# Keys and values stored to DRAM in 64-byte pieces, sorted by the partition that reads them, and loaded as 2 KB rows; chunk matmuls in two-bank tiles

## The chip, the cores and the metric

The kernel runs on one core of a Trainium2 chip. The metric is the device time of a run in microseconds (us). A separate execution was taken by the hardware profiler; its span is the time from its first to its last instruction.

## The reference

All arithmetic is float32. x is [64 batches, 64 tokens, 256]. Four layers, each with a residual, follow one another:

```python
x = x + L0(x, cond)      # adapter 256 -> 64 -> 256, weights scaled and shifted per batch
x = x + L1(x, cond)      # per batch a 256 -> 30 -> 256 product, U decoded from cond
x = x + L2(x, cond)      # attention among the 16 heads of ONE token
x = x + L3(x, ids, ...)  # gathered layer norms, hidden layer with silu, layer norm

# L2
kx = modulated_linear(x, s, k_aff_w, k_aff_b, k_w, k_b).reshape(B, N, 16, 16)
q = k = v = kx                                            # [b, token, head, d]
scores = einsum('bnhd,bnjd->bnhj', q, k) / sqrt(16)
out = einsum('bnhj,bnjd->bnhd', softmax(scores), v).reshape(B, N, 256)
out = modulated_linear(out, s, o_aff_w, o_aff_b, o_w, o_b)

# L3
h = ln(ln(x, pw_g[p], pw_b[p]), cp_g[c], cp_b[c]);  t = ln(x, tm_g[c], tm_b[c]);  s = ln(x, ms_g[m], ms_b[m])
# three more branches add per-batch vectors to x
y = ln(silu(concat(6 weighted branches) @ int_W1 + int_b1) @ int_W2 + int_b2, int_g, int_be)
```

The attention is between the heads of one token: each token has its own 16 x 16 score matrix.

## The kernel before

The 4096 tokens are taken in 8 chunks of 512 (`layers01`: layers 0 and 1 and the keys) and 16 units P of 256 (`attention` and `layers23`). x is held feature-major, 2 x 128 features on the partitions.

`layers01` runs stages "down" (tile p1 in PSUM), "up" (pu, evacuated by 16 small ScalarE operations into t1; pr, from which VectorE makes t2), "mid" (py, pz), "park" (x is written to DRAM as xd) and "keys" (pk, evacuated by 16 ScalarE operations into kT). Stage "turn" transposes kT (pt), and ScalarE copies it twice into the tile kk: once with the heads innermost (for the keys), once plainly (for the values). kk goes to DRAM as kd (L663).

`fetch` loads what the attention matmuls read. Eight tokens share a 128 x 128 matmul, 16 partitions (one for each d or head) for each token. kb holds keys of 8 tokens side by side; kz holds the same keys with gaps of zeros, so that each block of the product stays apart; vb holds values. kb and kz come in 8 + 8 DMAs of 16 x 32 pieces of 64 B (L679), vb in 8 such DMAs (L685). kb and vb have one buffer each, kz has two. "scores" multiplies kz by kb into pS (L707), VectorE and ScalarE make the softmax (mx, E, sm, at), "values" multiplies at by vb into pv (L731). ScalarE copies pv into av, four DMAs store it as ad (L743), one loads it back feature-major as aT (L747).

`layers23` scales aT (aS), multiplies (po, L794), scales on ScalarE (ot, 8 operations, L797) and adds the residual to xr, which was read back from xd. px (L805) transposes to token-major; ScalarE copies it to xt; VectorE makes statistics and the normalised branches in the order xh, pw, pw, statistics of pw, cg, mg, pw. POOL raises the variances to -1/2 and issues the gathers. pft, pfs, pfh (L830) transpose back, ph (L841, L843) is the hidden layer, pq (L851) its output, then a last layer norm and out.

PSUM has eight banks: tag A with two single banks for the chunk's tiles (taken in a fixed turn), tag B with three for layers23, S one for pS, V two for pv.

No order is written by hand. Each operation is a step with an engine, a cost, what it reads and writes, and a rank; `Plan.order` lets a list scheduler with modelled costs choose the order: among the steps of an engine that could start within 0.25 us of the earliest, the one of lowest rank. A step's rank is its unit's due time (25 us per P) plus a lead per stage (`LEAD`). All plain DMAs but W_dec and two small loads are on the SP queue, which issues them in that order and waits in that order.

Of the kernel before, what the change touches and what calls it, by code (L numbers as in the profile page):

```python
# [10 lines left out]
AF = mybir.ActivationFunctionType  # L11
# [5 lines left out]
HB = 64  # L17
# [44 lines left out]
class Plan:  # L62
# [3 lines left out]
    LANES, ISSUE, LAND, RATE, HOP, SLACK = 8, 0.57, 2.0, 280e3, 0.12, 0.25  # L66
    TABLE = 1.28

    LEAD = {"down": -39.4, "up": -8.6, "mid": -59.6, "keys": 28.3, "turn": 3.2, "fetch": 58.2,
            "scores": 59.6, "values": 68.7, "out": 41.8, "norm": -8.5, "hidden": 52.2, "last": 114.8,  # L70
            "gather": 86.4, "park": 50.6, "load": 74.1, "load first": -172.8, "load decoder": 56.9, "load up": -37.6,
            "load keys": 86.0, "load ids": -10.1, "load W1": -27.4, "load states": 22.4, "load W2": 20.8, "set down": -180.7,
            "set decoder": 123.4, "set k": -104.6, "set o": 113.5, "set W1": -81.6, "set states": 97.6}

    def __init__(self):
        self.stage = None
        self.steps, self.bufs, self.turn = [], {}, {}
        self.last_w, self.last_r = {}, {}

# [10 lines left out]
    def step(self, eng, cost, fn, r=(), w=(), rank=0.0, dma=None, table=None):  # L90
# [16 lines left out]
        for seen, mine in ((self.last_w, writes), (self.last_r, reads)):  # L107
            for name, part in mine:
# [3 lines left out]
                               stage=self.stage))  # L112
# [7 lines left out]
    def order(self):  # L120
        steps = self.steps
        n = len(steps)
        for s in steps:
            s["rank"] = s["base"] + self.LEAD.get(s["stage"], 0.0)
        users = {i: [] for i in range(n)}
# [18 lines left out]
        while placed < n:  # L144
# [44 lines left out]
            if s["dma"] is not None:  # L189
                pipe = max(pipe, t + cost + 0.8) + s["dma"] / self.RATE  # L190
                done[i] = max(t + cost + self.LAND, pipe + 1.0)
                if e != "POOL":
                    lanes.append(done[i])
# [29 lines left out]
def act(n, k=1):  # L223
    return 0.20 * k + n / 1250.0
# [3 lines left out]
def tile_kernel(ctx: ExitStack, tc: tile.TileContext, a: dict, out: bass.AP):  # L228
# [11 lines left out]
    BUFS = {"x": 3, "xr": 3, "pw": 2, "cg": 2, "mg": 2, "ei": 2, "oh": 2, "t4": 3, "kk": 2, "act": 2, "E": 2,  # L240
# [5 lines left out]
    def bank(name, tag="A", turns=False):  # L246
        return Buf(ps, tag, {"A": 2, "B": 3, "S": 1}[tag], [128, 512], name, turns=turns)
# [16 lines left out]
    onesz = fixed("onesz", [128, 2, 128])  # L264
# [31 lines left out]
    kb, vb = (kv[:, i * NG * 128 : (i + 1) * NG * 128].rearrange("p (g b j) -> p g b j", g=NG, b=8) for i in range(2))  # L296
# [3 lines left out]
    def consts():  # L300
        make_identity(nc, ident)

    step("POOL", 1.0, lambda: (nc.gpsimd.memset(ones, 1.0), nc.gpsimd.memset(onesz, 0.0),
                               nc.gpsimd.memset(onesz[0:HB, 0, :], 1.0), nc.gpsimd.memset(onesz[HB:128, 1, :], 1.0)),
         w=["ones", "onesz"], rank=-109)
# [247 lines left out]
    kds, xds = {}, {}  # L553

    def layers01(c, rank):
# [6 lines left out]
        p1 = bank(f"p1_{c}", turns=True)  # L562

        def f():
            for i in range(2):
# [15 lines left out]
        pu = [bank(f"pu_{c}_{h}", turns=True) for h in range(2)]  # L581
        step("PE", 0.9, lambda: [mm(pu[h]()[:, d * 256 : (d + 1) * 256], up2[h * HB : (h + 1) * HB, d * 128 : (d + 1) * 128],
                                    ac()[h * HB : (h + 1) * HB, :], start=True, stop=True) for d in range(2) for h in range(2)],
             r=[ac, "up2"], w=pu, rank=rank)
        for h in range(2):
            step("ACT", 8 * 0.31, lambda h=h: [
                nc.scalar.activation(t1()[:, d, h * 256 + b * S : h * 256 + (b + 1) * S], pu[h]()[:, d * 256 + b * S : d * 256 + (b + 1) * S],
                                     AF.Copy, scale=ugT[:, d, b0 + h * PB + b : b0 + h * PB + b + 1])
                for d in range(2) for b in range(PB)], r=[pu[h], "ugT"], w=[(t1, h)], rank=rank)
        pr = bank(f"pr_{c}", turns=True)  # L590
        step("PE", 0.9, lambda: [mm(pr()[:, h * 256 : (h + 1) * 256], onesz[:, h, :], ac(), start=True, stop=True) for h in range(2)],
             r=[ac, "onesz"], w=[pr], rank=rank)
        t2 = sb("t4", [128, 2, CH], f"t2_{c}")
        step("DVE", vec(1024), lambda: nc.vector.tensor_tensor(
            bt(t2()), over(pr().rearrange("p (b s) -> p b s", s=S), 2), rep(ubT[:, :, b0 : b0 + CB], S), ALU.mult),
            r=[pr, "ubT"], w=[t2], rank=rank)
# [4 lines left out]
        py = bank(f"py_{c}", turns=True)  # L601
# [10 lines left out]
        for h in range(2):  # L612
# [4 lines left out]
        pz = [bank(f"pz_{c}_{h}", turns=True) for h in range(2)]  # L617
        step("PE", 0.9, lambda: [mm(pz[h]()[:, d * 256 : (d + 1) * 256], V[h * HB : h * HB + K1P, d * 128 : (d + 1) * 128],  # L618
                                    y()[h * HB : h * HB + K1P, :], start=True, stop=True) for d in range(2) for h in range(2)],
             r=[y, "V"], w=pz, rank=rank)  # L620
        for h in range(2):
            step("DVE", vec(512), lambda h=h: nc.vector.tensor_tensor(
                x()[:, :, h * 256 : (h + 1) * 256], x()[:, :, h * 256 : (h + 1) * 256], pz[h]().rearrange("p (d t) -> p d t", d=2), ALU.add),
                r=[pz[h]], w=[(x, h)], rank=rank)
# [9 lines left out]
        kT = sb("t4", [128, 2, CH], f"kT_{c}")  # L634
        for o in range(2):
            pk = bank(f"pk_{c}_{o}", turns=True)
            step("PE", 1.75, lambda o=o, pk=pk: [mm(pk(), wT["k"][:, k, o * 128 : (o + 1) * 128], xs()[:, k, :], start=(k == 0), stop=(k == 1))  # L637
                                                 for k in range(2)], r=[xs, "w_k"], w=[pk], rank=rank)
            step("ACT", 8 * 0.31, lambda o=o, pk=pk: [
# [303 lines left out]
```

## Time and profile before

| | us |
|---|---|
| median of 3 runs (lowest to highest) | 538.52 (536.18 to 541.24) |
| the profiled execution | 543.12 |
| its span | 541.3 |
| first pS (scores of P=0) starts | 85.53 |
| first pft (hidden layer of P=0) starts | 129.24 |
| last pft (hidden layer of P=15) starts | 516.32 |

The lines of a profile read as follows. An engine's line gives its busy time, the share of the span and the number of instructions (PE is TensorE, PEld its weight loads, DVE VectorE, ACT ScalarE, POOL GpSimd). A DMA queue's line gives packets, MB, and the time that the packets took as a share of 16 DMA engines over the span. A line of the waits names the waiting engine, tile and line, then what released it, then total us, number of times and the longest. A line of the timeline gives start, duration, engine, line, operation, out<-in, shape and count; in brackets stands the engine's idle time before it and what ended that. SPq is the SP queue: the duration is that of the issuing instruction. Matmuls are pipelined, so that neighbouring durations overlap slightly. Line numbers are those of the kernel before; the changed kernel numbers its lines anew.

### The profile page before, as it was taken

To read this page: it belongs to the slowest core of one execution; us is meant where nothing else is said; L and a number is where in the kernel's file an instruction comes from. 1 tells how busy PE (TensorE), PEld (TensorE's weight loads), DVE (VectorE), ACT (ScalarE), POOL (GpSimd) and SP (SyncE) were. 2 spreads that over 40 slices of the span, in tenths; PEclk is the share of its full clock that TensorE was granted. 3 is DMA by queue.
4 is the path that set the end of the run, shared out by engine and by line. 5 is a ranking of instruction groups with operands and counts; after the bars stand their busy time and mean duration, and the time that the engine had idled before them with its cause. 6 is when DMAs were issued, how large, how long until landed. Compare 5 with 4: busy or idle time off the path is not lost.

```text
span 541.3 us, 10927 instructions
## 1 busy us (share of the span) xinstructions
PE 437.3 (81%) x4026; PEld 345.4 (64%) x4026; DVE 356.6 (66%) x778; ACT 244.6 (45%) x624; POOL 164.6 (30%) x181
## 2 busy tenths in 40 slices
PE   4976879677996998699899987999798869676481
PEld 3874446556775867477677676867676758665370
DVE  1653755258658785866859886797879494775532
ACT  1301532452557364825755576466647535251210
POOL 5380310003451515141425151515142424430100
PEclk9955986877999899979899999999999979796877
DMA  8994593656987697778687877878696869731000
GB/s 291 307 222 143 171 114 34 164 66 91 219 196 146 137 148 177 160 143 157 181 154 157 137 181 138 159 129 198 118 167 112 203 132 135 138 95 53 0 19 19
DMA packets 256994, 77.30 MB, mean 143 GB/s; under 512 B 226130, under 2 KB 242542, under 8 KB 256942
## 3 DMA queue, kind: packets, MB, share of 16 engines
q1 hardware_dynamic: 249006, 51.59, 48.9%
q0 software_dynamic: 6656, 20.98, 17.0%
q10 hardware_dynamic: 1280, 4.05, 2.0%
q8 instruction: 32, 0.52, 0.4%
q14 instruction: 20, 0.16, 0.1%
HBM read 55.60 MB, written 20.97 MB: 141 GB/s over the span
## 4 chain that ended last, share of the span: by engine, by line
PE 41%; SPq 22%; DMA 13%; DVE 12%; issue 6%; ACT 4%; POOL 1%; POOLq 0%; DVEq 0%; ACTq 0%
PE ph L843 12%; SPq L679 11%; PE pS L707 5%; DMA kd<-kk 4%; SPq L685 4%; PE po L794 4%; PE pq L851 3%; SPq L743 3%; PE pz L618 2%; DMA kz<-kd 2%; DMA aT<-ad 2%; DMA aff_k<-in_k_aff_wT 2%; PE pk L637 2%; PE ph L841 2%; PE pv L731 2%
## 5 line engine op out<-in xcount | busy, mean ns | idle before, releaser
L707 PE MATMUL pS<-kv,kz 128*32 128x128 f32 x1024 | 43.9, 343 | 33.1 <-DMA kz<-kd 21.5
L707 PEld LDWEIGHTS pS<-kv,kz 128*32 128x32 f32 x1024 | 38.7, 140 | 41.4 <-issue 31.0
L797 ACT ACTIVATE ot<-po,cols,demod_o 128x64 f32<-128x64 f32 x128 | 39.6, 417 | 30.3 <-PE po L794 30.3
L767 POOL DMA_INDIRECT mg<-in_ms_tab,ids x32 | 34.4, 1076 | 48.7 <-PE pfs L830 25.0
L757 POOL TENSOR_TENSOR rs_y<-rs_y,neghalf 128x2 f32<-128x2 f32 x16 | 12.6, 787 | 111.0 <-DVE rs_y L756 111.0
L757 POOL TENSOR_TENSOR rs_x<-rs_x,neghalf 128x2 f32<-128x2 f32 x16 | 12.7, 796 | 108.2 <-DVE rs_x L756 108.2
L640 ACT ACTIVATE kT<-pk,cols,demod_k 128x64 f32<-128x64 f32 x128 | 38.7, 440 | 7.7 <-PE pk L637 4.5
L833 ACT COPY ft<-pft 128x512 f32<-128x512 f32 x16 | 9.4, 585 | 72.1 <-PE pft L830 72.1
L767 POOL DMA_INDIRECT pw<-in_pw_tab,ids x32 | 33.3, 1040 | 10.4 <-issue 9.1
L767 POOL DMA_INDIRECT cg<-in_cg_tab,ids x32 | 32.5, 1015 | 11.3 <-issue 8.7
L843 PE MATMUL ph<-ft,W_t 128*128 128x256 f32 x128 | 35.6, 403 | 0.0
L854 DVE TENSOR_TENSOR y<-pq,irow 128x512 f32<-128x512 f32 x16 | 11.0, 688 | 35.8 <-PE pq L851 35.8
L790 DVE TENSOR_TENSOR aS<-aT,style_o 128x512 f32<-128x512 f32 x16 | 11.1, 691 | 34.8 <-DMA aT<-ad 34.8
L757 POOL TENSOR_TENSOR rs_h<-rs_h,neghalf 128x2 f32<-128x2 f32 x16 | 16.8, 1051 | 56.1 <-DVE rs_h L756 56.1
L794 PE MATMUL po<-aS,w_o 128*128 128x256 f32 x128 | 32.7, 401 | 0.9 <-DVE aS L790 0.9
L843 PE MATMUL ph<-xr,W_x 128*128 128x256 f32 x128 | 33.4, 383 | 0.0
L843 PE MATMUL ph<-fh,W_h 128*128 128x256 f32 x128 | 32.9, 380 | 0.0
L843 PE MATMUL ph<-fs,W_s 128*128 128x256 f32 x128 | 32.9, 379 | 0.0
L851 PE MATMUL pq<-W,hs 128*128 128x256 f32 x128 | 31.1, 385 | 1.8 <-ACT hs L846 1.7
L830 PE MATMUL pft<-ident,cg 128*128 128x128 f32 x64 | 12.3, 324 | 24.4 <-DVE cg L818 16.4
L731 PE MATMUL pv<-kv,at 128*32 128x128 f32 x1024 | 31.3, 274 | 0.8 <-issue 0.8
L637 PE MATMUL pk<-xs,w_k 128*128 128x512 f32 x64 | 31.0, 629 | 0.0
(217 smaller groups left out, 1020.9 us busy)
## 6 DMA issues: line engine op xcount, KB each, us to landing
kd<-kk SPq DMA_DIRECT2D x16, 512.0 KB
kv<-kd SPq DMA_DIRECT2D x256, 32.0 KB
x<-in_xT SPq DMA_DIRECT2D x8, 512.0 KB
xd<-x SPq DMA_DIRECT2D x8, 512.0 KB
xr<-xd SPq DMA_DIRECT2D x16, 256.0 KB
kz<-kd SPq DMA_DIRECT2D x128, 32.0 KB
ad<-av SPq DMA_DIRECT2D x64, 64.0 KB
aT<-ad SPq DMA_DIRECT2D x16, 256.0 KB
```

Source lines behind the costliest of these rows:

```text
L637: step("PE", 1.75, lambda o=o, pk=pk: [mm(pk(), wT["k"][:, k, o * 128 : (o + 1) * 128], xs()[:, k, :], start=(k == 0), stop=(k == 1)) for ...
L640: nc.scalar.activation(kT()[:, o, b * S : (b + 1) * S], pk()[:, b * S : (b + 1) * S], AF.Identity, scale=demod["k"][:, o, b0 + b : b0 + b ...
L679: nc.sync.dma_start(dst, bass.AP(k.tensor, k.offset + (q * 64 + l) * 2 * D, [[NH, HD], [2 * 2 * D, NG], [1, NH]]))
L685: nc.sync.dma_start(vb[b * 16 : (b + 1) * 16, :, b, :], bass.AP(k.tensor, k.offset + b * 2 * D + D, [[HD, NH], [8 * 2 * D, NG], [1, HD]]))
L707: mm(pS()[32 * cc : 32 * cc + 32, r * 128 : (r + 1) * 128], kzt[:, g * 32 + 16 : g * 32 + 48] if h == 0 else kzt[:, g * 32 : g * 32 + 32], ...
L731: mm(pv()[32 * q : 32 * q + 32, r * 2 + h, :], at_[:, c0 : c0 + 32], vb[:, q * 8 + h * 4 + r, :, :].rearrange("p b d -> p (b d)"), start=T ...
L757: step("POOL", 0.7, lambda: nc.gpsimd.tensor_tensor(rs(), rs(), neghalf[:, 0:2], ALU.pow), r=["neghalf"], w=[rs], rank=rank)
L767: step("POOL", 1.2, lambda dst=dst, tab=tab, i=i, t=t: nc.gpsimd.indirect_dma_start(out=dst()[:, t, :], out_offset=None, in_=a[tab], in_of ...
L794: step("PE", 1.74, lambda: [mm(po()[:, o * PT : (o + 1) * PT], wT["o"][:, k, o * 128 : (o + 1) * 128], aS()[:, k, :], start=(k == 0), stop ...
L797: step("ACT", 4 * 0.31, lambda o=o: [nc.scalar.activation(ot()[:, o, b * S : (b + 1) * S], po()[:, o * PT + b * S : o * PT + (b + 1) * S], ...
L843: mm(dst(), W1[n][:, k, o * 128 : (o + 1) * 128], rhs()[:, k, :], start=False, stop=(n == "h" and k == 1))
L851: step("PE", 0.87, lambda t=t: [mm(pq()[:, t * D : (t + 1) * D], hs()[:, k, t * 128 : (t + 1) * 128], W2[:, k, :], start=(k == 0), stop=(k ...
```

## The change

- kd becomes [d, token, head] and a new tensor vd [token mod 8, head, group, d] takes the values. Six DMAs store them in 64 B pieces: two for kd (one for each half of the tokens), four for vd.
- `fetch` loads kd once as a whole (kc, 128 rows of 2 KB), from which a ScalarE copy fills kz; kb and vb take 8 DMAs each of 16 rows of 2 KB. kb and vb are laid out block-major, so the matmuls read their moving operand as 8 pieces of 16 elements. The order of the tokens within a unit changes accordingly, and av and ad with it: ad's pieces are 128 B instead of 256 B.
- The two A banks become one tile of two banks for pu, pr, pz and pk. p1, py and pt move to the three B banks. pr multiplies only the 64 rows that it needs for each half; t2 is made in two halves.
- The scheduler's costs are new, its DMA model counts pieces, all `LEAD` numbers are new, and a table `SHIFT` adds an offset for each stage and unit.

```diff
-    LEAD = {"down": -39.4, "up": -8.6, "mid": -59.6, "keys": 28.3, "turn": 3.2, "fetch": 58.2,
...
+    LEAD = {"down": 461.1, "fetch": 587.4, "gather": 700.5, "hidden": 385.3, "keys": 522.6, "last": 599.3,
...
+    SHIFT = {"down": (16.6, 0.0, 113.0, 0.0, 97.7, 0.0, 91.0, 0.0, -9.0, 0.0, 7.5, 0.0, 47.7, 0.0, 9.6, 0.0),
...
-    kb, vb = (kv[:, i * NG * 128 : (i + 1) * NG * 128].rearrange("p (g b j) -> p g b j", g=NG, b=8) for i in range(2))
+    kb, vb = (kv[:, i * NG * 128 : (i + 1) * NG * 128].rearrange("p (b g j) -> p b g j", g=NG, b=8) for i in range(2))
...
-        pu = [bank(f"pu_{c}_{h}", turns=True) for h in range(2)]
+        pu = banks(f"pu_{c}")
...
-        step("PE", 0.9, lambda: [mm(pr()[:, h * 256 : (h + 1) * 256], onesz[:, h, :], ac(), start=True, stop=True) for h in range(2)],
+        step("PE", 0.45, lambda: [mm(pr()[:, h, 0:PT], onesq[h * HB : (h + 1) * HB, :], ac()[h * HB : (h + 1) * HB, :], start=True, stop=True)
...
-            kd = kds[P] = Buf(dram, "kd", 2 * NC, [PT, 2, D], f"kd_{P}")
-            step("SP", Plan.ISSUE, lambda kk=kk, kd=kd: nc.sync.dma_start(kd().rearrange("(t p) i f -> p t i f", p=128), kk()),
+            kd = kds[P] = Buf(dram, "kd", 2 * NC, [HD, PT, NH], f"kd_{P}")
+            vd = vds[P] = Buf(dram, "vd", 2 * NC, [8, NH, NG, HD], f"vd_{P}")
+            for t in range(2):
+                step("SP", Plan.ISSUE, lambda t=t, kk=kk, kd=kd: nc.sync.dma_start(
+                    kd()[:, t * 128 : (t + 1) * 128, :].rearrange("d p h -> p d h"),
+                    kk()[:, 0, t, :].rearrange("p (d h) -> p d h", h=NH)), ...)
+            for cc in range(4):
+                def f(cc=cc, kk=kk, vd=vd):
+                    src = bass.AP(src.tensor, src.offset, [[4 * k.ap[0][0], 32], [HD, 2 * NH], [1, HD]])
+                    nc.sync.dma_start(vd()[2 * cc : 2 * cc + 2].rearrange("l h g d -> g (l h) d"), src)
...
-                for dst, n in ((kb[b * 16 : (b + 1) * 16, :, b, :], "kb"), (kzv[b * 16 : (b + 1) * 16], f"kz{P % 2}")):
-                        nc.sync.dma_start(dst, bass.AP(k.tensor, k.offset + (q * 64 + l) * 2 * D, [[NH, HD], [2 * 2 * D, NG], [1, NH]]))
+        step("SP", Plan.ISSUE, lambda: nc.sync.dma_start(kc(), kd().rearrange("d (b g) h -> (d b) (g h)", b=8)), ...)
+        step("ACT", act(512), lambda: nc.scalar.copy(view(kz[z], [[32, NG], [1, NH]], 16), kc().rearrange("p (g h) -> p g h", h=NH)),
...
+                nc.sync.dma_start(bass.AP(dst.tensor, dst.offset, [[8 * dst.ap[0][0], HD], [1, NG * NH]]),
+                                  kd()[:, b * NG : (b + 1) * NG, :].rearrange("d g h -> d (g h)"))
...
-                nc.sync.dma_start(vb[b * 16 : (b + 1) * 16, :, b, :],
-                                  bass.AP(k.tensor, k.offset + b * 2 * D + D, [[HD, NH], [8 * 2 * D, NG], [1, HD]]))
+                vb[b * 16 : (b + 1) * 16, b].rearrange("p g d -> p (g d)"), vd()[b].rearrange("h g d -> h (g d)")),
...
-                           kb[:, g, :, :].rearrange("p b j -> p (b j)"), start=(h == 0), stop=(h == 1))
+                           kb[:, :, g, :], start=(h == 0), stop=(h == 1))
...
-                nc.sync.dma_start(bass.AP(t.tensor, t.offset + q * 64, [[HD * PT, NH], [PT, HD], [1, 64]]),
+                nc.sync.dma_start(bass.AP(t.tensor, t.offset + q * 32, [[HD * PT, NH], [PT, HD], [128, 2], [1, 32]]),
```

## The prediction

> **What bounds the kernel now.** I read the page first, then the waits, then the order of TensorE in time, then the windows of one steady chunk. The page:
>
> ```profile
> PE 437.3 (81%) x4026; PEld 345.4 (64%) x4026; DVE 356.6 (66%) x778; ACT 244.6 (45%) x624; POOL 164.6 (30%) x181
> ...
> DMA packets 256994, 77.30 MB, mean 143 GB/s; under 512 B 226130, under 2 KB 242542, under 8 KB 256942
> ...
> q1 hardware_dynamic: 249006, 51.59, 48.9%
> ```
>
> TensorE is busy 81% of 541.3 us and no engine is full, so waits decide. Nine of ten DMA packets are under 512 B: each of 16 units P fetches keys twice and values once, 3 x 4096 pieces of 64 B. The waits, longest of those that touch the fetch:
>
> ```profile
> PE pS L707 <- DMA kz<-kd: 21.5, 6, 5.7
> PE pft L830 <- DVE cg L818: 16.4, 7, 7.4
> ...
> SPq L679 <- DMA kd<-kk: 16.3, 7, 4.3
> ```
>
> The scores matmul waits 21.5 us for fetched keys, in six places. It is tempting to book all of it as gain. The order of TensorE shows why that is too much (start, duration, instruction; the bracket is idle before it):
>
> ```profile
> 358.41 0.66 PE L805 MATMUL px<-ident,xr 128*128 128x128 f32 x4
> ...
> 366.67 0.66 PE L830 MATMUL pft<-ident,cg 128*128 128x128 f32 x4 [1.70 <-DVE cg L818]
> ...
> 382.00 0.60 PE L805 MATMUL px<-ident,xr 128*128 128x128 f32 x4
> ...
> 388.69 1.95 PE L707 MATMUL pS<-kv,kz 128*32 128x128 f32 x64 [3.14 <-DMA kz<-kd]
> 390.58 1.13 PE L591 MATMUL pr<-act,onesz 128*128 128x256 f32 x4
> 391.54 0.60 PE L830 MATMUL pft<-ident,cg 128*128 128x128 f32 x4
> ...
> 409.33 0.66 PE L805 MATMUL px<-ident,xr 128*128 128x128 f32 x4
> ```
>
> A second loop runs through every P: px (transpose before the normalisation), a VectorE chain, pft, the hidden layer, po, ScalarE's ot, the next px. From px to pft the undisturbed VectorE chain takes 8.27 us (8.26, 8.27, 8.27, 8.27, 8.28 at five P). Whatever TensorE does in between is free up to 8.27. So the 3.14 us wait at 388.69 cost only 9.54 - 8.27 = 1.3 us. Over all P, px to pft reads 11.4, 14.7, 10.4, 9.5, 9.5 and 8.9 where a late fetch stands in it: 3.1 + 6.4 + 2.1 + 1.3 + 1.2 + 0.6 = 14.7 us above the floor. From pft to px it takes 15.3 to 15.7 us without a chunk's py and pz inside, 17.8 with them.
>
> At the start the order of SyncE decides instead. pv of P=0 starts at 94.01 and po of P=0 only at 113.45, since its output goes through SP behind a row of fetches:
>
> ```profile
> 98.97 2.44 SPq L685 DMA_DIRECT2D kv<-kd  x4
> ...
> 102.08 2.65 SPq L743 DMA_DIRECT2D ad<-av  x4
> ...
> 106.25 2.04 SPq L685 DMA_DIRECT2D kv<-kd  x3
> 108.47 0.38 SPq L747 DMA_DIRECT2D aT<-ad  x1
> ```
>
> The windows of one chunk (two P), 337 to 391 us, show DMA 78% busy; SP's rows in that window add up to 46.9 of 54 us.
>
> **What the Trainium skill says.** "DMA: Bandwidth & Descriptors", Specifications: under 512 B a transfer isn't at line rate, the engine does read-modify-write. The trace's packet records of before have no 64 B store. They have 196,736 packets of 64 B, nearly all fetches (11.0 ns each), 16,736 of 256 B, nearly all stores of ad (16.5), and 8,192 of 2 KB (93). The 256 B stores lie on the line between the others, so no penalty is seen there. Same page, Queues, rings and completion order: SP owns one ring on each DMA engine, consumed in ring order. So a small load waits behind stores issued before it. "TensorE: Matmul & The Clock Gate", The HAM clock gate: an idle window of about 3.4 us halves the clock. The trace agrees: pS took 3.64 us after 5.68 us idle at 231.40, 1.95 us undisturbed.
>
> **The change part by part.**
>
> *Loads.* Per P, 24 fetches of 512 packets become kc (128 rows of 2 KB) and 8 + 8 fetches of 16 rows. Between kd landed and the last key fetch issued lie 16 issues now, 322.57 to 334.5 = 12 us with stalls; after, 9 issues at about 0.43 us (the median of kd, also few descriptors) = 4 us. kz is then filled by a ScalarE copy of 128x512, 16 x 0.59 us (row of av: 0.599) = 9.4 us on an engine 45% busy. Where kc is late, this copy holds up ft or av behind it on ScalarE.
>
> *Stores.* kd was one DMA of 256 x 2 KB. Now two of 2048 and four of 1024 packets of 64 B, 8192 per P. Their price is unseen: below, 8 ns (the lowest tenth of the 64 B records); above, three times a fetch, 33 ns. I take 11 ns, since ad's stores show no penalty. ad goes from 1024 x 256 B to 2048 x 128 B; 12.8 ns each by the line. Per chunk: -8192 x 11 - 2048 x 16.5 + 4096 x 12.8 + 256 x 93 ns = -48 us of one engine, -3.0 us of sixteen. DMA per chunk goes from 42 (0.78 x 54) to 39 us.
>
> *SP.* Per chunk: 34 small issues x 0.43 = 14.6; 12 stores, if SP is held as long as their packets run, 16384 x 11 / 16 = 11.3; ad 8 x 0.65 = 5.2; the rest 4. That is 35 us against 46.9.
>
> *Order.* New LEAD and SHIFT numbers change every queue. In the instruction order of the changed kernel, pt_0 of a chunk now stands a whole P and more ahead of the pS that reads its keys (pt_0 and the pS have a hidden layer, po, pq, pv, px, pS of the P before, and another hidden layer between them). Before it was 11 us (377.71 to 388.69). py and pz of chunks 3 to 7 move from the hidden layers of P=2,4,..10 to P=1,3,..9. So store and load latency is covered even at double price; what is late next is px to pft, the VectorE chain.
>
> *PSUM.* pu, pr, pz, pk become one two-bank tile used in turn; p1, py, pt go to the three B banks with po, px, pf, ph, pq. pr follows both ScalarE passes over pu (3.4 us), but has pS and pt or p1 before it. pr's matmuls use half the rows each: 1.0 to about 0.5 us, 4 us in all, mostly inside the 8.27. t2 in two halves: 2 x 0.69 against 1.22 on VectorE, 1.3 us in all. For B banks taken late I put 5 us in all (0 to 12; the analogue is pq's 1.68 us wait for hs at 430.93).
>
> *Strided matmul operands.* kb and vb are now read as eight pieces of 16 elements. pg already reads condT in short pieces at 0.11 us a matmul, not dearer than its neighbours. I take 0; if it doubled pS and pv, 2 x 1.95 x 16 = 62 us, which nothing supports.
>
> *The sum.* Head: pk of chunk 0 now starts at 52.59; py of chunk 0 and p of chunk 2 stand ahead of it, so 54. From there to pft of P=0 the new order has 53 us of TensorE work by the rows of before (pk 3.6 three times, pS 3.6 + 2 x 1.95, pbt 7.7, po 1.9, pv 2 x 1.9, the small ones the rest). Before takes 76.6 us for nearly the same; its excess of some 23 is the waits of pS (3.3 and 3.2), the ad path and the slow clock. Of that I leave 7: pft of P=0 at 114 instead of 129.24, 15 less. Body: 15 x 8.27 + 10 x 15.5 + 5 x 17.8 = 368 instead of 387.1 (129.24 to 516.32), 19 less. Tail: 25.0, unchanged; its gaps are the VectorE chain. New stalls +5. 114 + 368 + 25 + 5 = 512 us span. The profiled execution took 543.12 us for a span of 541.3, so 514; the median of the runs is 538.52 / 543.12 = 0.9915 of it: 510 us.
>
> **Rivals.**
> 1. Only the body gains: the head stays (SP now sends kd, vd and fetches of two P before the first ad), or new stalls of 15 us come. Span 541.3 - 15 = 526, runs 522. For it: the new head has 9 large stores before kc of P=0. Against: TensorE has 10 us of other work there.
> 2. No change: what the fetch frees is taken by bank waits and ScalarE copies in the 8.27 us loop. 538. Against: ScalarE has half its time free.
> 3. Slower: 64 B stores cost more than fetches. With c ns per packet, DMA per chunk is 39 + 1.02 x (c - 11). It passes the new loop (49.8) at c = 21.5 and the old period (52.9) at 24.6; from there the kernel is slower. At 28 ns: 56.4 per chunk, 6.5 chunks x 3.5 = +23, head gain lost: span 564, runs 561. For it: DMA is already 93% busy in 340.66 to 358.41, and the page's remark on read-modify-write. Against: ad's stores.
>
> **How the numbers follow.** Forecast 510 (498 to 522): 0.64. Rival 1: 0.17. Rival 2: 0.06. Rival 3: 0.13. A measurement here tells about 1% from no change. Faster 0.81, same 0.06, slower 0.13. The low end, 494, is the forecast without new stalls and 10 us more in the head; the high end, 540, takes in rivals 1 and 2 and leaves rival 3 outside.
>
> **What would show it.** Right: no wait of pS for a DMA over 1 us in the body; px to pft at 8.3 us in nearly every P; pft of P=0 near 114; DMA share per chunk near 39 us; 64 B packets 131,000 at about 11 ns. Wrong: 64 B stores above 21 ns; SP rows of kd and vd of several us with ad behind them; ScalarE idle before the kz copy; TensorE waiting for a B bank.

## The result, and the profile after

The changed kernel is slower: 558.69 us (median of 4 runs, 557.27 to 563.48) against 537.35 us for the kernel before on the same chip. The ratio is 1.040, with a 95% interval of 1.032 to 1.049. The prediction was 510 us, with a chance of 0.81 for faster. The profiled execution took 557.27 us, its span 555.5. Some runs of a kernel fall into a slower state: medians here are of all its runs, ratios are of its fast runs to fast runs of the kernel before on the same chip.

From the page after, and then from its waits (total, number of times, longest):

```profile
PE 437.4 (79%) x4026; PEld 341.6 (62%) x4026; DVE 363.7 (65%) x786; ACT 252.2 (45%) x640; POOL 169.0 (30%) x179
...
q1 hardware_dynamic: 201390, 51.58, 46.2%
```

```profile
PE pft L869 <- DVE cg L857: 43.5, 12, 7.9
...
PE pz L645 <- DVE y L640: 7.7, 5, 2.4
PE ph L880 <- ACT ft L872: 6.5, 6, 2.1
```

TensorE's busy time is the same to a tenth of a microsecond; VectorE and ScalarE are busy 7 to 8 us longer. The fetch did become cheaper: the queue of all plain DMAs has 48,000 fewer packets and a smaller share. The wait that the change was made for, pS for fetched keys, 21.5 us before, is off the head of the list. What has grown is pft's wait for VectorE (16.4 before) and pz's for y (1.6 before), and ph's for ft is new. So TensorE's work is no more than before, and most of the time went into the order of things around it.

It can be put into places with the same two stretches as in the prediction, px to pft and pft to px:

| us | before | predicted | after |
|---|---|---|---|
| pft of P=0 starts | 129.2 | 114 | 127.2 |
| px to pft, sum over P=1 to 15 | 139.0 | 124.1 | 125.4 |
| pft to px, sum over P=0 to 14 | 248.1 | 244.0 | 277.6 |
| from pft of P=15 to the end | 25.0 | 25.0 | 25.4 |

The gain in px to pft came as forecast, 13.6 us. The stretch with the hidden layer, for which I had booked a small gain, lost 29.5 us. TensorE in P=9, in order of time (start, duration, instruction; the bracket is idle time before it):

```profile
373.33 0.70 PE L617 MATMUL pr<-act,onesq 64*128 64x256 f32 x4 [1.01 <-ACT t L613]
376.46 0.66 PE L869 MATMUL pft<-ident,cg 128*128 128x128 f32 x4 [2.43 <-DVE cg L857]
...
378.40 1.91 PE L882 MATMUL ph<-ft,W_t 128*128 128x256 f32 x4
...
384.00 1.03 PE L882 MATMUL ph<-ft,W_t 128*128 128x256 f32 x4
...
388.41 1.58 PE L645 MATMUL pz<-y,V 32*128 32x256 f32 x8 [1.31 <-DVE y L640]
```

Three things are to be seen. TensorE idles 1.01 and 2.43 us ahead of pft. After it the first group of ph on ft takes 1.91 us, the second one, the same four instructions, 1.03. And pz, which has only one ph group between itself and py, waits for y. In P=4, 6, 8 and 10 there is a fourth thing: ph waits 1.27 to 1.42 us for ft.

### The profile page after: what moved, and what is told of

It reads as the page before. It is cut to its first block, busy times and chain, and to the rows that moved or that the text cites. A ratio compares the mean times of both kernels' runs of the same rounds, so it can differ in the third digit from the quotient of the medians.

```text
span 555.5 us, 10987 instructions
## 1 busy us (share of the span) xinstructions
PE 437.4 (79%) x4026; PEld 341.6 (62%) x4026; DVE 363.7 (65%) x786; ACT 252.2 (45%) x640; POOL 169.0 (30%) x179
## 4 chain that ended last, share of the span: by engine, by line
PE 48%; DVE 17%; ACT 10%; DMA 9%; SPq 7%; issue 5%; another core or an unknown queue 2%; POOL 1%; POOLq 0%; DVEq 0%; ACTq 0%
PE ph L882 18%; PE po L833 5%; ACT kT L667 4%; PE pq L890 3%; PE pk L664 3%; ACT ot L836 3%; PE pv L770 3%; PE ph L880 3%; PE p L594 2%; PE pS L746 2%; PE pz L645 2%; DMA aff_k<-in_k_aff_wT 2%; DMA res_W<-in_res_W 2%; SPq L719 1%
## 5 line engine op out<-in xcount | busy, mean ns | idle before, releaser
L869 PE MATMUL pft<-ident,cg 128*128 128x128 f32 x64 | 12.5, 328 | 51.6 <-DVE cg L857 43.5
L806 POOL DMA_INDIRECT mg<-in_ms_tab,ids x32 | 37.0, 1155 | 34.3 <-PE pfs L869 12.9
L869 PEld LDWEIGHTS pft<-ident,cg 128*128 128x128 f32 x64 | 8.2, 164 | 58.5 <-issue 49.4
L806 POOL DMA_INDIRECT cg<-in_cg_tab,ids x32 | 35.3, 1102 | 19.6 <-DVE ys_noi L549 6.6
L882 PE MATMUL ph<-ft,W_t 128*128 128x256 f32 x128 | 40.3, 445 | 0.0
L885 ACT ACTIVATE hs<-ph,cols 128x256 f32<-128x256 f32 x32 | 15.1, 473 | 54.4 <-PE ph L882 47.3
L882 PE MATMUL ph<-fs,W_s 128*128 128x256 f32 x128 | 35.1, 398 | 0.0
L746 PE MATMUL pS<-kv,kz 128*32 128x128 f32 x1024 | 31.3, 274 | 3.4 <-DMA kv<-vd 1.9
L770 PEld LDWEIGHTS pv<-kv,at 128*32 128x32 f32 x1024 | 28.6, 114 | 7.9 <-issue 3.8
L796 POOL TENSOR_TENSOR rs_x<-rs_x,neghalf 128x2 f32<-128x2 f32 x16 | 13.6, 848 | 64.6 <-DVE rs_x L795 64.6
L882 PEld LDWEIGHTS ph<-ft,W_t 128*128 128x128 f32 x128 | 29.3, 229 | 5.7
L746 PEld LDWEIGHTS pS<-kv,kz 128*32 128x32 f32 x1024 | 27.0, 110 | 8.5 <-issue 7.6
```

The costliest lines, as they stand in the source:

```text
L746: mm(pS()[32 * cc : 32 * cc + 32, r * 128 : (r + 1) * 128], kzt[:, g * 32 + 16 : g * 32 + 48] if h == 0 else kzt[:, g * 32 : g * 32 + 32], ...
L770: mm(pv()[32 * q : 32 * q + 32, h * 4 + r, :], at_[:, c0 : c0 + 32], vb[:, :, q * 8 + h * 4 + r, :], start=True, stop=True)
L796: step("POOL", 0.7, lambda: nc.gpsimd.tensor_tensor(rs(), rs(), neghalf[:, 0:2], ALU.pow), r=["neghalf"], w=[rs], rank=rank)
L806: step("POOL", 1.2, lambda dst=dst, tab=tab, i=i, t=t: nc.gpsimd.indirect_dma_start(out=dst()[:, t, :], out_offset=None, in_=a[tab], in_of ...
L869: step("PE", 0.45, lambda s=s, pf=pf: [nc.tensor.transpose(pf()[:, k * PT + t * 128 : k * PT + (t + 1) * 128], s()[:, t, k * 128 : (k + 1) ...
L882: mm(dst(), W1[n][:, k, o * 128 : (o + 1) * 128], rhs()[:, k, :], start=False, stop=(n == "h" and k == 1))
```

## The experiments

The theory: the new data path does what it was meant to, and the time is lost by what came with it, in three places (A1 a PSUM tile of two banks, A2 the place of pz, A3 a cold TensorE clock, that is, one that runs at half speed after idle time). A4 (ScalarE's kz copy) and A5 (the order on SP) came up later. The rival, B: the data path itself costs the time, through 64 B stores, short operand pieces or the extra copies.

### The first four: one cause each

**split_banks** keeps the changed kernel's order on every engine and makes each two-bank tile as two tiles in the same two banks.

```diff
-        mm(pk()[:, o, :], wT["k"][...], xs()[:, k, :], ...)
+        mm(pk(o), wT["k"][...], xs()[:, k, :], ...)       # pk(0), pk(1): one bank each; pu, pr, pz likewise
```

> The changed kernel with its own order on every engine, but each two-bank PSUM tile (pu, pr, pz, pk) made as two tiles of one bank in the same two banks. Theory A1 (a two-bank tile is one thing to wait for: kT starts 3.8 us after the first pk matmul in the changed kernel and 2.0 in the one before): kT starts 1.8 us sooner, the four waits of ph on ft (1.27 + 1.34 + 1.42 + 1.42 = 5.5 us) go, and the head gains up to 2: 549 to 554 us against some 558.5. Rival (the tile's form costs nothing; kT is late because pS stands ahead of pk): within 2 us of 558.5, the ph waits still there.

Measured: 544.53 us, ratio to before 1.013 (1.005 to 1.021). Keys of chunk 7 in the changed kernel, then keys of chunk 6 in split_banks, each with the pft and the ft copy after them, from TensorE's and ScalarE's order in time:

```profile
399.65 3.70 PE L664 MATMUL pk<-xs,w_k 128*128 128x512 f32 x8
...
403.45 4.84 ACT L667 ACTIVATE kT<-pk,cols,demod_k 128x64 f32<-128x64 f32 x16 [4.50 <-PE pk L664]
...
405.72 0.63 PE L869 MATMUL pft<-ident,cg 128*128 128x128 f32 x4 [2.37 <-DVE cg L857]
...
408.09 0.67 ACT L872 COPY ft<-pft 128x512 f32<-128x512 f32 x1
```

```profile
334.93 3.70 PE L675 MATMUL pk<-xs,w_k 128*128 128x512 f32 x8
...
337.01 4.85 ACT L678 ACTIVATE kT<-pk,cols,demod_k 128x64 f32<-128x64 f32 x16 [2.79 <-PE pk L675]
...
341.00 0.63 PE L880 MATMUL pft<-ident,cg 128*128 128x128 f32 x4 [2.38 <-DVE cg L868]
...
341.67 0.67 ACT L883 COPY ft<-pft 128x512 f32<-128x512 f32 x1
```

In the changed kernel kT starts 3.80 us after pk, when both halves are done; with a tile for each bank 2.08 us after, as before (2.0). ScalarE is then free for ft when pft ends, ft starts 0.67 us after the start of pft instead of 2.37, and ph's waits on ft of over 1 us are gone. The gain, 14 us, is more than the 5 to 9 expected. pft to px falls by 15.3 us, but 9.0 of these lie in P=0 and 1, and most of them are not the tiles' (see below). From pft of P=2 to the end the traces differ by 6.3 us, as expected.

**pz_late** moves pz behind the last ph group in the five P where it stood between them.

```diff
+        for c in range(3, 8):
+            order = later(order, pz of chunk c, behind the last ph of P = 2c - 5)
```

> The changed kernel with pz moved behind the last ph group, in the five P where it stood between ph groups. Theory A2 (pz stands too close behind py): its waits on y, 2.30 + 2.37 + 1.26 + 1.31 = 7.2 us, go and nothing takes their place, 550 to 554 us. Rival (the x update, xs and pk are then late, or the hidden layer's end is set by ScalarE): 557 to 560 us.

Measured: 553.92 us, ratio 1.034 (1.026 to 1.041). 4.8 us, near the low end of the expected gain. P=1 falls from 23.57 to 17.97 us, but P=3 and 6 grow by 1.5 and 2.1, and px to pft of P=2 by 3.6. From pft of P=2 to the end this trace is 0.9 us longer than that of the changed kernel, so a loss by the place of pz is not shown.

**warm** puts matmuls whose result nobody reads ahead of pft. They go into pft's own bank, which pft overwrites.

```diff
+            warm = (0, 0, 0, 3, 1, 1, 1, 2, 1, 2, 1, 4, 5, 5, 7, 7)[P] if n == "t" else 0
-            step("PE", 0.45, lambda ...: [nc.tensor.transpose(pf()[...], ...) ...])
+            step("PE", 0.45, lambda ...: [mm(pf(), W2[:, 0, 0:128], W2 as 512 columns, start=True, stop=True) for _ in range(warm)]
+                                         + [nc.tensor.transpose(pf()[...], ...) ...])
```

> The changed kernel with dummy matmuls of 512 columns put ahead of pft, into pft's own bank, where TensorE idles there (1 in P 4, 5, 6, 8, 10; 2 in P 7, 9; 3 in P 3; 4, 5, 5 in P 11 to 13; 7 in P 14 and 15). Theory A3 (TensorE's clock is cold after the idle time: the first ph<-ft group takes 1.91 us instead of 1.03, the hidden layer 10.6 to 11.9 instead of 9.3 to 9.5): 1.3 to 2 us in each of P 3, 7, 9 and 11 to 15, the layer back at 9.3 to 9.6 in P 11 to 15, 544 to 551 us. Rival (ScalarE's copies of ft, fs and fh set these 1.91 us, or the extra work is throttled): 557 to 562 us.

Measured: 539.95 us, ratio 1.002 (0.995 to 1.008), a gain of 18.7 us, more than expected; from pft of P=2 to the end the traces differ by 14.1 us. P=13 of the changed kernel, then P=12 of warm, TensorE in order of time:

```profile
480.24 1.09 PE L869 MATMUL pft<-ident,cg 128*128 128x128 f32 x4 [5.60 <-DVE cg L857]
...
481.97 1.06 PE L880 MATMUL ph<-oh,bigtab 72*128 72x256 f32 x2
```

```profile
442.32 4.56 PE L870 MATMUL pft<-W 128*128 128x512 f32 x10
447.79 0.66 PE L871 MATMUL pft<-ident,cg 128*128 128x128 f32 x4 [0.92 <-DVE cg L857]
...
448.90 0.60 PE L882 MATMUL ph<-oh,bigtab 72*128 72x256 f32 x2
```

The same pft takes 1.09 us after 5.60 us of idle time and 0.66 after the dummies, ph<-oh 1.06 and 0.60. In P=11 to 14 pft to px falls from 16.2–17.1 us to 14.5–14.9. TensorE does 4.56 us of useless work there and the kernel gets faster. The Trainium skill ("TensorE: Matmul & The Clock Gate", HAM oscillation) describes this failure, waits between short bursts that throttle the clock again and again. The trace agrees, as the profile's record of the granted clock shows. Its half-speed stretches are 3.41, 6.83, 10.24 us and so on long, whole multiples of one window, which is as long as the page's Part 1 gives it. Four such windows of the changed kernel, two around pft of P=8 (351.21) and two around pft of P=9 (376.46): stretch, its length, TensorE's busy time and instructions, granted clock (1.00 or 0.50), DMA share and GB/s:

```profile
346.82:350.24 3.42, 2.02 (x5) 1.00 0.51 134
350.24:353.65 3.41, 1.73 (x12) 1.00 0.36 71
374.14:377.55 3.41, 1.09 (x8) 1.00 0.89 163
377.55:380.96 3.41, 3.41 (x12) 0.50 0.96 162
```

The idle time before pft is the same, 2.37 and 2.43 us. In P=8 it falls into two windows, each busy for half its length or more, and the clock stays up. In P=9 it falls into one, busy for a third, and the next window has half the clock. The section's rule, no idle gaps over about 3.4 us, is thus too mild for this kernel: 2.43 us were enough.

**A difference that belongs to no edit.** The dummies of warm begin at P=3, yet its P=1 takes 17.72 us instead of 23.57, and P=0 1.7 us less. Up to pft of P=2 TensorE has the same instructions in the same order in both kernels. P=1 of the changed kernel, then of warm, from TensorE's and VectorE's order in time:

```profile
161.24 1.09 PE L635 MATMUL py<-x,U 128*32 128x64 f32 x32
165.22 0.86 DVE L640 TENSOR_TENSOR y<-py,ubias 32x256 f32<-32x256 f32 x2 [1.61 <-remote]
165.69 2.52 PE L645 MATMUL pz<-y,V 32*128 32x256 f32 x8 [2.30 <-DVE y L640]
```

```profile
159.53 1.09 PE L635 MATMUL py<-x,U 128*32 128x64 f32 x32
160.87 0.85 DVE L640 TENSOR_TENSOR y<-py,ubias 32x256 f32<-32x256 f32 x2
161.60 1.30 PE L645 MATMUL pz<-y,V 32*128 32x256 f32 x8
```

In the changed kernel's trace VectorE starts y 2.89 us after the end of py, though it is idle for the last 1.61 of them; in that of warm 0.26 us after. pz waits, the clock drops (165.92 to 172.75 at half speed), and pz takes 2.52 us instead of 1.30. In six of the 17 traces (before, the changed kernel, before_warm, all_three, all_kz, head) an idle VectorE starts y of chunks 3 to 7 1.0 to 3.7 us after py; in the other eleven after at most 0.23 us. The cause is open; since kernels with the same order fall into both groups, it goes with the execution and not with the edit. So the 5.6 to 5.9 us that P=1 gains in each of split_banks, pz_late and warm are not shown to be the edits', and px to pft of P=2 gives most of them back (8.84 us in the changed kernel, 13.44, 12.46 and 14.57 in the three). The dummies' own gain is sure where no py or pz stands any more: from px of P=11 to the end warm is 10.5 us shorter. pft to px of P=11 to 14 sums to 66.6 us in the changed kernel, to 67.7 and 67.0 in split_banks and pz_late, where y is on time, and to 58.9 in warm.

**layout_old_order** is the other way round: before's kernel, with only the data path changed.

> The kernel before with only the data path of the change: sorted stores, 2 KB row loads, the ScalarE copy kc to kz, the two pieces of av; one-bank PSUM tiles, the old priorities and costs stay, so that TensorE's order in the body is that of before. Theory A (the data path does what it was meant to, the new order and the two-bank tiles lose the time): the pS waits go, which are 139.0 - 15 x 8.27 = 14.9 us of before's px-to-pft stretches; a cold TensorE clock may take up to 4 back; 522 to 531 us, ratio 0.970 to 0.988 to before. Theory B (the data path itself is what costs: 64 B stores, strided operands, the extra copies): the pft-to-px stretches grow here too, 550 to 562 us, ratio 1.02 to 1.05.

Measured: 571.75 us, ratio 1.057 (1.049 to 1.066). This is neither what theory A nor what B said in its working: the pft-to-px stretches grew (283.8 us), but not by 64 B stores or operands. Most pS and pv take the 1.96 us of before for their 64 matmuls. Of the 283.8 us TensorE has half the clock for 43.0. The other groups that grew are waits, from the view of the waits of ScalarE and of TensorE:

```profile
ACT kz L686 <- DMA kc<-kd: 38.4, 14, 7.0
```

```profile
PE py L608 <- DVE x L598: 19.9, 5, 5.9
```

The copy that fills kz stood at the head of ScalarE's queue waiting for its DMA, with ot or ft behind it. So A as it stood fell: in both orders tried the data path brings a wait of its own (15.5 us in five waits in the changed kernel). The next two groups follow the two sides.

### Is the loss before's own, and do the three add up?

**before_warm**: the same dummies in the kernel before (1 in P=3, 5, 7, 9, 11; 7 in P=14 and 15).

> The kernel before with the same dummy matmuls ahead of pft, where TensorE idles over 1 us there (1 in P 3, 5, 7, 9, 11; 7 in P 14 and 15): how much of the gain of warm is the change's own loss. Theory A3 (before paid for a cold clock in P 5, 14 and 15 alone, 1.6 us each): 530 to 535 us, ratio 0.985 to 0.995. Rival (dummies gain as much in any kernel, 15 us or more): 525 us or less, and then the cold clock explains nothing of the change's loss.

Measured: 541.65 us, ratio 1.000 (0.995 to 1.006): no gain that can be measured. In the changed kernel the dummies took the ratio from 1.040 to 1.002. So the cold clock is a loss of the change, not of the kernel as such. The record of the granted clock shows why. From the first pft to the last TensorE has half the clock for 49.2 us in before and for 60.4 us after, not much longer. But in before 38.2 us of it lie between px and pft, where TensorE waits for VectorE anyway, and 11.0 between pft and px, where its own work counts; after, 15.6 and 44.9 us. In warm the 44.9 are 11.7. In before other matmuls stood right ahead of pft in nine P (0.4 us idle or less; after, in two). In six of these it was, among others, a pS that came late: by the order, a wait that looked like pure loss did a service. That it was pS, and not the other matmuls there, was not tested.

**all_three**: one-bank tiles, pz late and the dummies.

> The changed kernel with the one-bank tiles, pz behind the last ph group, and the dummy matmuls together. If the three losses are separate: 558.5 - 18.6 - 14 - 4.6 = 521 us; where they overlap (pz's wait and the clock in the same P) 522 to 530. If one loss was behind all three: 538 to 544 us, no better than the best alone.

Measured: 538.94 us, ratio 0.997 (0.993 to 1.001), no better than warm alone. pft to px: 277.6 after, 262.3, 270.9 and 259.6 in the three alone, 257.1 in all together. The three don't add up, in part since P=0 and 1 stand in all three gains (9.0, 7.3 and 7.5 us) and are mostly not theirs. Part is given back: y is late here again (2.6 to 3.7 us), and P=12 takes 22.26 us here (14.76 in warm), as po waits 4.78 us for aS. Behind that stands ScalarE's kz copy once more: it waits 6.05 us for kc, ahead of av, and so ad, aT and aS are late.

### The kz copy and its buffer

Two kernels move the kz copy back in ScalarE's queue, behind the copies of px and pv that precede the pS which needs it.

```diff
+        for P in range(1, 16):
+            order = later(order, kz copy of P, behind ScalarE's last xt or av copy ahead of pS of P)
```

> The kernel with before's order and the new data path (571.75 us), where ScalarE's copy of kc into kz is moved back in ScalarE's queue, behind the copies of px and pv that precede the pS that needs it. Theory A4 (the copy stood at the head of ScalarE's queue waiting for its DMA, 38.4 us in 14 waits, right ahead of ot and ft; behind it the chain ot, xr, px and the chain t1, x, py were late by 7.2 and 19.9 us): most of these go, 543 to 553 us; what is then left over before is the cold clock. Theory B (the data path costs through DMA or operands): 562 us or more.

> The former with ScalarE's copy of kc into kz moved back in its queue too, in ten of the P. If its waits (15.5 us in five in the changed kernel) lie on the path: 2 to 6 us below the former. Rival (most of these waits fall where ScalarE has time): within 1.5 us of the former; if pS is then late, up to 4 above.

Measured: layout_kz_late 584.24 us (1.079, 1.066 to 1.093), all_kz 554.19 us (1.019, 1.003 to 1.035). Both got worse. SP's queue in all_kz shows why, and TensorE in P=10, with the longest of these waits (384.43 to 394.95) ahead of it:

```profile
SPq L748 <- ACT kz L750: 25.0, 4, 10.5
```

```profile
402.05 3.64 PE L783 MATMUL pS<-kv,kz 128*32 128x128 f32 x64 [7.75 <-DMA kv<-kd]
```

kc has one buffer. SP stops at the load of the next kc until the copy has read the last one; all other loads and stores stand behind, and pS waits for its keys. Moving a wait off one queue had put it on another. In layout_kz_late this is not seen: SP waits 8.8 us for the copy, at stores of kd and ad, and why that kernel got worse is open. The next two kernels are the same with two buffers for kc (the second in space that only the start uses):

```diff
         kc = kcs[P] = sb("kc", [128, NG * NH], f"kc_{P}")
+        if P % 2:
+            kc.place = "s_wsq"
```

> As all_kz (one-bank tiles, pz late, dummies, the kz copy late in ScalarE's queue), but with two buffers for kc in turn. In all_kz SP waited 25.0 us, four times, for the kz copy, since the next load of kc writes the one buffer that the copy still reads. Theory A4' (the copy's place was right, the one buffer of kc was what cost): SP's waits on kz gone, and P 12's wait of po on aS (4.78 us in all_three, behind a kz copy that waited 6.05 us for kc ahead of av) gone too: 528 to 535 us, under all_three's 539. Rival (loads of kc and kb land late anyway): 539 to 552 us.

> As layout_kz_late (before's order, new data path, kz copy late; 584 us) with two buffers for kc. Theory A4': SP is no longer held by the kz copy (some 9 us of its waits in layout_kz_late), 562 to 574 us. What then stays above before is VectorE's wait of aS for aT (9.1 us in P 4), behind which the x update and py stand. Rival (SP's hold did not matter): 578 to 588 us.

Measured: all_kz2 532.54 us (0.989, 0.968 to 1.010), layout_kz2 569.90 us (1.060, 1.046 to 1.074). Both fell where theory A4' (the one buffer was the cost) had them, by 21.7 and 14.3 us. In all_kz2 SP's waits for the copy are gone, and px to pft of P=10 takes 8.41 us instead of 16.99: this much the buffer is shown to be worth. pft to px falls from 260.2 to 246.0, against 244.0 predicted for the change, but 10.8 of these 14.2 us lie in the five P with a py, where y came late in all_kz and not in all_kz2. P=12 is back at 14.76 us in both. For layout_kz2 the theory's sign is missing: SP still waits 7.8 us for the copy, and 7.2 of the 10.5 us that its span lost are P=0, where y had come 4.8 us late.

### What is left in before's order: SP's slots

layout_kz2 still loses 28.0 us in py's wait for x. In front of x VectorE holds aS, which waits for aT (VectorE's waits; then SP's queue in P=4, where pft starts at 230.12):

```profile
DVE aS L829 <- DMA aT<-ad: 41.4, 9, 10.0
```

```profile
223.53 3.00 SPq L691 DMA_DIRECT2D kd<-kk  x2
226.62 3.31 SPq L699 DMA_DIRECT2D vd<-kk  x4
...
231.67 3.66 SPq L782 DMA_DIRECT2D ad<-av  x4
...
239.70 0.37 SPq L786 DMA_DIRECT2D aT<-ad  x1
```

Two stores of kd and four of vd take 6.3 us to issue, and ad stands behind them with its data ready at 225.5. In before one store of kd took 0.60 us in this place, and aT went out at 235.46, 1.3 us ahead of pft (236.80); here 9.6 us after it. Two kernels change SP's order.

```diff
-  SP:  kd x2, vd x4, kc, vb x2, ad x4, vb x4, aT, vb x2
+  SP:  kd x2, kc, vb x2, ad x4, vd x4, aT, vb x6           # layout_sp
+  SP:  kd x2, ad x4, vd x4, kc, aT, vb x8                  # layout_ad
```

> As layout_kz2, and on SP the four stores of vd are moved behind the ad stores that follow them, and four loads of vd behind the load of aT. Theory A5 (in before's order SP's slots are the limit: four vd stores, 4.6 us of issue, stand ahead of ad, so aT lands some 5 us late and aS, at the head of VectorE's queue, holds the x update and py): aT 3 to 5 us sooner in P 4, 6, 8, 10, aS's waits shrink by as much, 10 to 18 us below layout_kz2: 548 to 560 us. Rival (the 16 queues are full, ad's and aT's packets come late whatever their place): within 4 us of layout_kz2.

> As layout_kz2 (before's order on TensorE, new data path, kz copy late, two kc buffers; 570 us), and on SP the four ad stores moved ahead of everything between the kd stores and them: the vd stores, the load of kc and the first loads of vd; the other loads of vd stand behind the load of aT. Theory A5 (SP's slots): in P 4 ad then goes out at 226.6 instead of 231.7 and aT some 5 us sooner; VectorE's wait of aS for aT (41.4 us in nine) and TensorE's of py for x (28.0 in five) shrink by half or more: 548 to 558 us. Rival (full DMA queues): within 4 us of 570, or above.

Measured: layout_sp 594.90 us (1.110, 1.096 to 1.124), layout_ad 566.62 us (1.045, 1.035 to 1.056). layout_sp failed for a reason that I had not seen: the vd stores had covered the time in which the load of kc waits for the kd stores ahead of it to land. Without them SP waits (12.8 us in four, none listed in layout_kz2), and aT's wait on SP for ad to land grows from 8.9 to 23.9 us. layout_ad does what A5 says to aS and moves the wait on (VectorE's and TensorE's waits):

```profile
DVE aS L839 <- DMA aT<-ad: 21.3, 8, 7.0
```

```profile
PE pS L756 <- DMA kc<-kd: 11.4, 1, 11.4
```

aS's waits halve, aT goes out 6.1 us after pft instead of 9.6, but kc, now behind ad and vd, lets pS of one early P wait 11.4 us. pft to px falls by 12.9 us, px to pft grows by 5.5 and the head by 4.7. That SP's slots matter is shown; the sum is 3.3 us, too little for the expected 12 to 22. A good SP order for this data path with before's TensorE order was not found, and whether there is one is open.

> The former with dummy matmuls ahead of pft (1 in P 3 to 11, 4 in P 12 and 13, 7 in P 14 and 15). Theory A3: 5 to 10 us below the former. Rival (the clock matters only in the new order): within 2 us of it.

Measured: 560.73 us (550.46 to 564.82) against 566.62 (560.88 to 572.7). The ranges overlap, so this one is undecided as a whole. In its trace P=12 to 14 fall from 16.2–17.6 us to 14.5–14.8, as in warm, with y on time in both traces.

### The last waits, and the head

**best_p_late** takes all_kz2 and moves two p (layer 0 of later chunks) from ahead of pft to behind the next px.

> As all_kz2 (one-bank tiles, pz late, dummies, kz copy late, two kc buffers; 532.5 us), with p of chunk 5 moved from ahead of pft of P 2 to behind px of P 3, and p of chunk 7 from ahead of pft of P 5 to behind px of P 6. There px to pft took 14.4 and 13.1 us instead of 8.3, p of chunk 7 waiting 3.1 us for its x. If nothing else stands there: 525 to 530 us, ratio to before 0.970 to 0.985. Rival (pS, waiting 3.6 us for kb in P 2, holds pft anyway): 530 to 534 us.

Measured: 535.68 us (22 runs) against 537.61 for before (27 runs), ratio 0.991 (0.987 to 0.995). The 95% interval excludes a ratio of 1: this repaired version beats the kernel before, by 0.9%, and the changed kernel. It is no gain over all_kz2 that can be told apart; px to pft sums to 134.0 (134.3 there): P=2 fell from 14.36 to 10.76 us, but P=3 grew from 8.10 to 11.78, now full of p and dummies, and in P=6, at 13.18, pS waits 2.68 us for kz. From its page and waits:

```profile
PE 465.7 (88%) x4106; PEld 349.7 (66%) x4106; DVE 362.8 (68%) x786; ACT 251.5 (47%) x640; POOL 168.1 (32%) x179
```

```profile
PE pft L913 <- DVE cg L899: 12.5, 10, 2.6
PE pS L788 <- DMA kv<-kd: 5.0, 2, 3.0
```

**head** moves p of two chunks behind the first pk, and pS of P=2 behind pfh of P=0.

> As best_p_late (535.7 us), with three steps moved at the start: p of chunk 1 behind the first pk, p of chunk 2 behind pt, pS of P=2 behind pfh of P=0. There p of the two chunks took 5.9 us at the slow clock ahead of pk (58.74), and pS 1.9 us ahead of pft of P=0 (125.37). If TensorE's order sets the head: pk at 53 to 55, pft of P=0 at 119 to 122, 3 to 6 us off the whole, ratio to before 0.980 to 0.987. Rival (pS and po wait for data behind SP's row of loads: pS of P=0 waited 3.1 us for values, po 1.4 for aS): pk earlier, but the first pS and po where they were; pft of P=0 at 123 to 125, within 2 us of best_p_late.

Measured: 547.37 us, ratio 1.019 (1.010 to 1.028): neither side had that. As the rival says, an earlier pk brings nothing. pk came 1.7 us sooner (57.08, after 4.35 us idle), the first pS at 85.34 instead of 83.91, pft of P=0 at 126.40 instead of 125.37. P=0, with pS in the middle of its hidden layer, took 22.08 us instead of 15.19. Another 7.1 us lie in P=1, 3, 5, 7 and 9, far from the edit, where y came late in head and not in best_p_late. SP's row at the head of the changed kernel, where pv of P=0 is done at 94.9 and av at 98.24:

```profile
89.23 4.95 SPq L719 DMA_DIRECT2D kv<-kd  x8
...
98.27 3.19 SPq L782 DMA_DIRECT2D ad<-av  x4
101.56 2.32 SPq L693 DMA_DIRECT2D kd<-kk  x2
103.97 1.62 SPq L701 DMA_DIRECT2D vd<-kk  x2
105.76 0.57 SPq L786 DMA_DIRECT2D aT<-ad  x1
```

ad goes out as soon as av is there, but aT only at 105.76, behind stores of kd and vd; before it was 108.47. That this row holds the head is a reading of the order and was not tested.

## Why the prediction was wrong, step by step

- **Loads: right.** px to pft reads 8.0 to 8.9 us in every P from 1 to 15, sum 125.4 for 124.1. DMA's share of a steady chunk (351.2 to 405.7) is 0.66 of 54.5, 36 us; 39 were predicted.
- **Stores: right, and with them rival 3 is refuted.** The 131,200 packets of 64 B, now all but 128 of them stores, took 11.5 ns on average (11.0 before, when they were loads). The 32,768 of 128 B took 11.4; 12.8 were predicted. The kernel is slower, as that rival said, but not by its mechanism.
- **Operands in short pieces: right.** 1.95 us for pS and pv, as before.
- **The body, pft to px: the step that failed.** "10 x 15.5 + 5 x 17.8" took the durations of before's rows as properties of the instructions. They were properties of before's order, and even there P=5, 11 and 14 took 17.0, 17.1 and 16.5 us. 277.6 us came instead of 244.0, with 44.9 us at half clock instead of 11.0. Two causes are shown: the cold clock (10.5 us behind px of P=11 alone) and the two-bank tile (6.3 us behind pft of P=2, and 7.2 against pz_late, which has such tiles and y on time). A loss by the place of pz is not shown; the waits of pz that theory A2 counted go with a late y, whose cause is open. With all of these and the kz copy repaired, and y on time, the stretch measures 246.0.
- **PSUM, "B banks taken late": the wrong stall was named.** The price of 5 us stood for banks of layers23. What came was a tile of two banks that lets ScalarE start 1.8 us later in seven of the eight chunks. The kernel's text showed it: pk was two tiles, one for each half, and kT's first eight operations read only the first half.
- **"Whatever TensorE does in between is free up to 8.27": right for work, wrong for its absence.** I cited the clock gate for a slow pS, and did not ask what a TensorE that waits for nothing but VectorE would do to the clock. The change removed late pS waits and left pft behind 2.0 to 7.9 us of idle time in twelve P.
- **ScalarE copy of kz: priced by its duration alone.** 9.4 us of work on a half-idle engine was near (10.6). The wait at the head of an in-order queue was named, but with no price. It was 15.5 us in five waits after, and 38.4 in before's order. I had not seen that the one buffer of kc links it to SP.
- **SP: neither the sum nor the places.** SP's rows in the steady chunk (351.2 to 405.7) add up to 43.3 us, where 35 were predicted and before has 46.9. Between 130 and 520 us a store of kd takes 1.11 us and one of vd 1.12 to issue, where before one of kd took 0.47. In before's order they come in a block of six with ad behind it; in the changed kernel's own order ad goes first, and in six P aT stands behind three or four of them. Rows of several us with ad behind them were on my list of what would prove me wrong.
- **Head: the second step that failed**, 127.2 for 114. I gave TensorE's order and the freed SP 15 us. The first half of rival 1 was right on it ("the head stays"). Its reason, SP's row, fits the trace and was not tested. Two executions with the same instructions up to there, before and before_warm, have pft of P=0 at 129.2 and 123.5, so the 2 us to before say nothing.
- **Sum.** 13.2 for the head, 33.6 for pft to px, 1.3 for px to pft, 0.4 for the tail, less the 5 of stalls that the sum contained, are 43.5 us: from 512 to the measured span of 555.5.

The best version shows what the change is worth. Its body has nearly the pft to px of the forecast (247.5 us), but px to pft sums to 134 instead of 124, as pS waits about 3 us for keys in P=2 and 6 and P=3 is full of work, and the head keeps 11 us over the forecast. Of a forecast gain of 28 us, about 5 are left by the ratio.

## What to carry to other kernels

Durations read from a trace hold for the order in which they were taken: before a wait is removed, ask what it keeps warm, covers or spaces out. An instruction that waits for a DMA costs what stands behind it on its in-order queue, and moving it helps only if its buffer doesn't move the wait to the queue that refills it. Where a tile is joined or split, look for the reader that needed only half of it.

## What the runs showed of the hardware

- The granted clock changes on a grid of 3.41 us. The skill's page says that the window runs free of the program, and the traces agree: the grid begins 1.24 us after the first instruction in before, 2.08 in the changed kernel and 2.76 in warm. In the changed kernel's trace 15 full-speed windows were followed by one at half speed, and TensorE was busy for 0 to 45% of each; of those followed by another at full speed, all but three were busy for 44% or more. So 2.4 us of idle time ahead of pft cooled the clock in P=7 and 9, where one window took most of it, and not in P=8 and 10, where two shared it. After 4.4 us and more it was cold in every P.
- A cold clock cost nothing where TensorE waited for VectorE. Before has it for 49.2 us, 38.2 of them between px and pft; dummies cut the 49.2 to 35.5, and the time stayed. In the changed kernel 44.9 of 60.4 us lie between pft and px, and there dummies paid.
- Useless matmuls can pay: 1 to 7 of 0.9 us each ahead of pft, with nothing else changed, go with 3.7% off the changed kernel (1.040 to 1.002; at least 10.5 us of it are theirs) and nothing off the kernel before.
- Stores in packets of 64 B and of 128 B cost the same for each packet, 11.5 and 11.4 ns, and 64 B loads 11.0 (before). Ad's packets of 256 B took 16.5 ns (before).
- Issuing a DMA is not a fixed price for SP. The median for a vd store of 1024 packets is 0.75 us, the longest 2.4, in the changed kernel; in all_three four of them took 8.28 us in a row.
